# A second engine that fetches rows by plain DMAs in a message-passing kernel

## The chip, the cores and the metric

The kernel runs on one core of a Trainium2 chip. A core has a matrix engine (TensorE, PE in the profile), VectorE (DVE), ScalarE (ACT), GpSimd (POOL) and SyncE (SP), each with an instruction queue of its own that it works off in order, and sixteen DMA engines that they share. SBUF is the on-chip memory of 128 partitions, PSUM the memory that PE writes into.

The metric is the time of one execution on the device in microseconds. Before the change it is 3964.24 us, the median of three runs (3958.78 to 3966.85).

## The reference

One layer of a graph network over 12500 nodes and 400000 edges, sorted by their destination. A node has 64 scalars and 32 vectors of three components. For each edge, the rows of the source node are fetched, weighted by a small network of the edge's own 64 features, combined with four edge attributes and summed at the destination:

```python
h_s = s @ lin1_ws * a * _inv(S_IN)
h_v = jnp.einsum('nci,cd->ndi', v, lin1_wv) * a[:, :, None] * _inv(V_IN)
hid = jax.nn.silu(edge_scalars @ fc_w1 * _inv(R))
w = hid @ fc_w2 * _inv(FC_HID)
w1, w2, w3, w4, w5 = jnp.split(w, [64, 128, 160, 192], axis=-1)
es = h_s[edge_src]
ev = h_v[edge_src]
...
m_s1 = w1 * es * e0
m_s2 = w4 * jnp.einsum('eci,ei->ec', ev, e1) * _inv(3)
m_v1 = (w2 * es)[:, :, None] * e1[:, None, :]
m_v2 = w3[:, :, None] * ev * e0[:, :, None]
m_v3 = w5[:, :, None] * jnp.cross(ev, e1[:, None, :]) * _inv(2)
...
agg_s = jax.ops.segment_sum(mid_s, edge_dst, num_segments=n) * inv_nn
agg_v = jax.ops.segment_sum(mid_v, edge_dst, num_segments=n) * inv_nn
```

The sums go through a second linear map, a gate and a layer norm with the node's own row added.

## The kernel before

**Tiles and steps.** The 400000 edges are 3125 tiles of 128, one edge in each partition. A step works on a quad of four tiles; there are 782 steps. Six steps are a chunk of 24 tiles, whose 64 features per edge are loaded by SyncE in two DMAs (`load_chunk`, line 200, tile `es`). Ahead of the loop the table `h_tab` of 12500 rows, 160 floats or 640 bytes each, is computed and written to the chip's HBM.

**Where the rows come from.** `gather` (line 464) issues one indirect DMA per tile from GpSimd, 128 rows by the tile's indices, into `hg`, a tile for a quad out of a pool of four buffers (`deep`). For every 68th step from step 76 on, eleven in all (`own`, line 473), the rows come another way: `places` (line 477) loads the quad's indices as four rows of 128 into `at_bytes`, VectorE multiplies them by 640 (line 746), and `rows_of` (line 486) makes 32 jobs, each of which loads sixteen of these byte addresses into SyncE's registers (line 492) and issues sixteen DMAs of one row each (line 497) into `hq`, which has one buffer. `fetch_rows` (line 740) issues one job at every second step, so 32 jobs take 64 steps, and the quad is used by the step that they were made for.

**The order.** The scheduler is told to keep each engine's instructions in the order in which the code writes them, so the loop at line 874 is the order of every queue. In a step it issues: the loads that are due (`fetch`, for the quad four steps ahead), `fetch_rows`, the gather of this step, the matmuls of the edge weights into `pw` (line 510), a transposition for finished nodes if one is due (line 646), the one-hot rows of destinations (line 573), the products (lines 520 and 528, tile `pr`), the selection matrices (line 582, `sel`), the sums of the quad two steps before (`sum_up`, line 589, into `pa`), the first layer of the edge network for the quad two steps ahead (`hide`, line 459, and ScalarE's silu, line 461, tile `hid`), the second linear map of finished blocks (`output`, lines 613 and 616), and the transposition of summed blocks (`turn_blocks`, lines 598, 601 and 603, tile `tt`).

**What ScalarE does.** It copies a pair of finished blocks out of `pa` (line 795, tile `sa`, turned two steps later), the silu, the copies of `tt` and `os`, the reordering of edge attributes (line 556), the tanh and the square root of finished nodes (lines 648 and 673), and in steps 2 to 9 it clears the accumulator `acc` (line 433, two pieces a step). The PSUM tiles `ph`, `pt`, `po`, `pp` and `psc` take turns in two banks named `misc`; `pw` and `pa` have two buffers each.

**Finished nodes.** 25 jobs in the loop, of four tiles of 128 nodes each, and one behind it load `x`, turn the sums, gate, normalise and store (`finish`); the store is SyncE's (line 682) and waits for VectorE's `y` (line 679).

The functions that the diff touches:

Of the kernel before, what the change touches and what calls it, by code (L numbers as in the profile page):

```python
# [10 lines left out]
F32 = mybir.dt.float32  # L11
I32 = mybir.dt.int32
# [6 lines left out]
ENG = mybir.EngineType  # L19
PSUM = bass.MemoryType.PSUM  # L20

P = 128
# [3 lines left out]
D = S + V3  # L26
# [6 lines left out]
Q = 4  # L33
# [4 lines left out]
NF = 4  # L38
OWN = 68
BATCH = 16  # L40
EVERY = 2

MARGIN = 128
NO = 16
# [13 lines left out]
def gnn_kernel(  # L58
# [21 lines left out]
    nc = tc.nc  # L80
    N = x.shape[0]
# [19 lines left out]
        engines={ENG.PE, ENG.DVE, ENG.Activation, ENG.Pool, ENG.SP}))  # L101
# [33 lines left out]
    steps = []  # L135
# [92 lines left out]
    with tc.tile_pool(name="nodes", bufs=len(starts)) as nodes, tc.tile_pool(  # L228
        name="nodes_ps", bufs=6, space=PSUM
# [49 lines left out]
        for i in range(2):  # L279
            r = slice(S + i * V, S + (i + 1) * V)  # L280
# [23 lines left out]
        for half in range(2):  # L304
            r = slice(half * S, (half + 1) * S)
# [14 lines left out]
        for c0, cn, quarters, cq, xa, xz in loaded:  # L320
# [4 lines left out]
            first = c0 // P  # L325
            full = cn // P
            for t0 in range(0, nt, U):
                ps = nps.tile([P, U, P], F32, name="hp")
                for t in range(t0, min(t0 + U, nt)):
                    n = min(P, cn - t * P)  # L330
                    nc.tensor.matmul(ps[:n, t - t0], xa[:, t * P:t * P + n], l1,
                                     start=True, stop=True)
                k = min(U, full - t0)
# [3 lines left out]
                if t0 + k < nt <= t0 + U:  # L337
                    n = cn - full * P
# [4 lines left out]
            r = slice(0, P) if quarters == 4 else slice(S, S + V)  # L343
            by = l1z if quarters == 4 else l1[r, r]
            for u in range(-(-cq // P)):
                n = min(P, cq - u * P)
# [10 lines left out]
            if cn > full * P:  # L357
                n = cn - full * P
# [19 lines left out]
    for half in range(2):  # L378
        r = slice(half * S, (half + 1) * S)
# [21 lines left out]
    for to, part, pieces, w, r0, c0, by in maps:  # L401
        for k, piece in enumerate(pieces):
# [3 lines left out]
            m = terms.setdefault((to, part, four), len(terms))  # L406
            at_r = at_p * V
            r = l2[at_r:at_r + V, m, c0:c0 + w.shape[1]]
# [61 lines left out]
                in_offset=bass.IndirectOffsetOnAxis(ap=i, axis=0))  # L470
        return hg

    own = [n for n in range(OWN + 8, len(steps) - 4, OWN) if len(steps[n][2]) == Q]
    by_bytes = h_tab.rearrange("n d -> (n d)").bitcast(U8)
    row_bytes = 4 * D

    def places(pool, n):

        at_bytes = pool.tile([Q, P], I32, name="at_bytes")
        for k, (t, _, _) in enumerate(steps[n][2]):  # L480
            g, u = divmod(t, GT)
            with nc.allow_non_contiguous_dma(reason="the indices of one tile"):
                nc.sync.dma_start(at_bytes[k:k + 1], src[g][:, u:u + 1].rearrange("p u -> u p"))
        return at_bytes

    def rows_of(pool, at_bytes):

        hq = pool.tile([P, Q, D], F32, name="hq", bufs=1)
        flat_hq = hq.rearrange("p t d -> p (t d)").bitcast(U8)

        def job(t, p0):
            _, values = nc.values_load_multi_w_load_instructions(
                at_bytes[t:t + 1, p0:p0 + BATCH], engines=[ENG.SP], min_val=0,
                max_val=(N - 1) * row_bytes,
                skip_runtime_bounds_check_because="every entry of src is the index of a node")
            for p, v in enumerate(values, p0):
                nc.sync.dma_start(flat_hq[p:p + 1, t * row_bytes:(t + 1) * row_bytes],
                                  by_bytes[ds(v, row_bytes)][None])

        return hq, [lambda t=t, p0=p0: job(t, p0) for t in range(Q) for p0 in range(0, P, BATCH)]  # L500

    def weights(psum, hid, slots):

# [120 lines left out]
    def finish(fin, psum, t0, nt, p, most=NF):  # L624
# [50 lines left out]
        def norm():  # L675
# [14 lines left out]
    jobs = [(t, min(NF, tiles_of_nodes - LAST - t), P)  # L690
            for t in range(0, tiles_of_nodes - LAST, NF)]
    last_job = (tiles_of_nodes - LAST, LAST, N - (tiles_of_nodes - 1) * P)

    with tc.tile_pool(
        name="fin", bufs=1
    ) as fin, tc.tile_pool(
        name="mine", bufs=2
    ) as mine, tc.tile_pool(
        name="late", bufs=2
    ) as late, tc.tile_pool(name="edge", bufs=2) as edge, tc.tile_pool(  # L700
        name="deep", bufs=4
# [33 lines left out]
                for t, _, _ in tiles:  # L735
                    ahead(t)

        at_of, hq_of, rows_due = {}, {}, []

        def fetch_rows(n):  # L740

            for m in own:
                if n == max(1, m - OWN - 6):
                    at_of[m] = places(mine, m)
                if n == m - OWN + 2:
                    nc.vector.tensor_scalar_mul(at_of[m], at_of[m], float(row_bytes))
                    hq_of[m], jobs = rows_of(mine, at_of[m])
                    rows_due.extend((m, job) for job in jobs)
            if n % EVERY == 0 and rows_due:
                rows_due.pop(0)[1]()  # L750
            assert all(m > n for m, _ in rows_due)

        def hide(n):

# [112 lines left out]
        with in_order:  # L867
# [6 lines left out]
            for n, (c, i, tiles) in enumerate(steps):  # L874
# [5 lines left out]
                if n in checks:  # L880
                    checks[n]()
                fetch(n + 4)
                fetch_rows(n)
                hg = hq_of.pop(n) if n in own else gather(deep, [index(t) for t, _, _ in tiles])
                pw = weights(pw_ps, hids[c, i // 2], [(half, u - i // 2 * 4) for _, half, u in tiles])
# [34 lines left out]
            n = len(steps)  # L920
# [29 lines left out]
        with tc.For_i(0, n_redo, 1):  # L950
# [9 lines left out]
            with tc.For_i(0, n_again, 1) as g, tc.For_i(0, GT, 1) as k:  # L960
                t = g * GT + k
# [22 lines left out]
                r = edge.tile([P, 1], F32, name="r", bufs=1)  # L984
# [8 lines left out]
                first = nc.values_load(ends[0:1, 0:1], min_val=0, max_val=N - 1)  # L993
# [65 lines left out]
```

## Time and profile before

| | |
|---|---|
| median of three runs | 3964.24 us |
| profiled execution | 3954.57 us |
| its span, first to last instruction | 3952.6 us |
| mean granted TensorE clock | 0.969 |
| moved by DMA | 412.50 MB |
| GpSimd's gathers | 3081 |
| SyncE's DMAs of one row | 5632 |

The profile is of one execution. Its page gives busy time by engine; groups of instructions by line, with the count, the busy time, the mean length of one in ns and the idle time of the engine just before them with what ended it; other views list waits, the instructions in order of time, busy time by stretch, and the instructions of one line with their shortest, median and longest time. PEld is the weight load of PE. An engine name with a q (SPq, ACTq) is the engine's sequencer, which issues DMAs, loads registers and waits; that time is not counted as busy. A releaser of "issue" means that the engine waited for nothing that the profile shows.

### The profile page before, as it was taken

Reading aid. Unit: us, or ns where it says so; the run is one execution under the profiler, and the core shown is the slowest. Engines: PE = TensorE matmul, PEld = TensorE weight load, DVE = VectorE, ACT = ScalarE, POOL = GpSimd, SP = SyncE. Lnnn points to the kernel's source line nnn. Section 1 sums busy time; section 2 is a strip of 40 time slices with the busy share of each in tenths; the row PEclk is TensorE's granted clock in tenths of the full one; section 3 lists DMA queues with packets and bytes.
Section 4 is the critical chain, followed back from the end, with each engine's and each line's share of the span. In section 5 each row is a group of like instructions: output and inputs, shape, how many; then the busy total and the mean of one; then the engine's idle time right before and its main releaser. Section 6 shows DMA issues by size and latency. Waiting matters only on the chain. (4 is left out here: it accounts for less than half of the span.)

```text
span 3952.6 us, 58252 instructions
## 1 busy us (share of the span) xinstructions
PE 3649.2 (92%) x14269; PEld 1584.2 (40%) x14269; DVE 2415.6 (61%) x6524; ACT 894.0 (23%) x2480; POOL 2929.3 (74%) x3100
## 2 busy tenths in 40 slices
PE   5899999999999999999999999999999998999997
PEld 4343343343444344334344344344343443344343
DVE  5656565665665665656656656666665665666665
ACT  1322222222222222222222222222221221222222
POOL 4777777777777777777777777777777777777774
PEclk8999999999999999999999999999999999999999
DMA  8443444444444444344443443444443444444442
GB/s 230 97 103 90 108 105 96 108 103 105 100 96 110 103 97 108 95 116 96 102 110 86 110 110 89 108 100 100 108 106 90 109 103 105 100 100 108 100 109 55
DMA packets 243192, 412.50 MB, mean 104 GB/s; under 512 B 83069, under 2 KB 173497, under 8 KB 241945
## 3 DMA queue, kind: packets, MB, share of 16 engines
q0 software_dynamic: 150160, 262.93, 27.3%
q1 hardware_dynamic: 92246, 145.66, 15.8%
q8 instruction: 115, 1.88, 0.2%
q14 instruction: 235, 1.93, 0.2%
q10 hardware_dynamic: 436, 0.10, 0.0%
HBM read 392.43 MB, written 16.00 MB: 103 GB/s over the span
## 5 line engine op out<-in xcount | busy, mean ns | idle before, releaser
L468 POOL DMA_INDIRECT hg<-h_tab,idx x3081 | 2915.0, 946 | 949.5 <-issue 846.7
L510 PE MATMUL pw<-w,hid 128*128 128x448 f32 x3126 | 1363.3, 560 | 119.1 <-DVE sel L582 78.2
L589 PE MATMUL pa<-pr,sel 128*64 128x416 f32 x6250 | 1302.2, 539 | 3.1 <-DVE pw L573 2.9
L528 DVE TENSOR_TENSOR pr<-pw,hg 128x384 f32<-128x384 f32 x2313 | 1136.9, 547 | 0.0
L520 DVE TENSOR_TENSOR pr<-pw,hg 128x512 f32<-128x512 f32 x771 | 532.7, 691 | 876.8 <-DMA hg<-h_tab,idx 623.1
L510 PEld LDWEIGHTS pw<-w,hid 128*128 128x128 f32 x3126 | 555.2, 194 | 595.2 <-issue 461.6
L589 PEld LDWEIGHTS pa<-pr,sel 128*64 128x64 f32 x6250 | 388.0, 139 | 814.0 <-issue 803.6
L795 ACT COPY sa<-pa 128x416 f32<-128x416 f32 x521 | 263.3, 505 | 1205.7 <-PE pa L589 1190.5
L573 DVE TENSOR_TENSOR pw<-rel,iota 128x64 f32<-128x64 int16 x782 | 179.6, 230 | 543.5 <-PE pw L510 541.2
L459 PE MATMUL misc<-es,w 128*128 128x512 f32 (+1 forms) x784 | 450.2, 656 | 26.8 <-DVE rel L421 21.6
L461 ACT ACTIVATE hid<-misc 128x512 f32<-128x512 f32 x392 | 233.5, 596 | 778.4 <-PE misc L459 778.1
L598 PEld LDWEIGHTS misc<-ident,sa 128*128 128x128 f32 x2084 | 240.2, 141 | 318.7 <-issue 267.8
L613 PE MATMUL misc<-tt,l 128*96 128x256 f32 (+5 forms) x1474 | 343.6, 380 | 6.6 <-DVE y L659 6.0
L598 PE MATMUL misc<-ident,sa 128*128 128x128 f32 x2084 | 328.4, 280 | 8.3 <-DVE acc L776 3.8
L582 DVE TENSOR_TENSOR sel<-pw,eas 128x256 f32<-128x256 f32 x782 | 322.8, 413 | 0.0
L613 PEld LDWEIGHTS misc<-tt,l 128*96 128x96 f32 (+1 forms) x1474 | 225.2, 162 | 142.5 <-issue 73.9
L601 ACT COPY tt<-misc 128x192 f32<-128x192 f32 x521 | 164.7, 316 | 501.9 <-PE misc L598 482.6
L459 PEld LDWEIGHTS misc<-es,w 128*128 128x128 f32 x784 | 119.6, 192 | 293.8 <-issue 238.5
L621 DVE TENSOR_TENSOR acc<-acc,os 96x32 f32 x1042 | 194.6, 187 | 28.0 <-ACT os L616 9.6
L646 PE MATMUL misc<-ident,acc 96*128 96x96 f32 x196 | 36.6, 272 | 97.1 <-DVE pw L573 67.9
L603 ACT COPY tt<-misc 128x64 f32<-128x64 f32 x521 | 117.1, 225 | 0.0
L616 ACT COPY os<-misc 96x512 f32<-96x512 f32 (+2 forms) x67 | 38.2, 569 | 293.4 <-PE misc L613 286.7
(86 smaller groups left out, 608.6 us busy)
## 6 DMA issues: line engine op xcount, KB each, us to landing
es<-in_es_t_dram SPq DMA_DIRECT2D x258, 384.0 KB
hq<-h_tab SPq DMA_DIRECT2D x5632, 0.6 KB
hg<-h_tab,idx POOLq DMA_INDIRECT x3081
h_tab<-ht POOLq DMA_DIRECT2D x6, 1280.0 KB
xt<-in_x_dram SPq DMA_DIRECT2D x23, 320.0 KB
out_dram<-y SPq DMA_DIRECT2D x23, 320.0 KB
xv<-in_xv_t_dram SPq DMA_DIRECT2D x25, 187.5 KB
xs<-in_xs_t_dram SPq DMA_DIRECT2D x25, 125.0 KB
```

The source lines that it names most:

```text
L459: nc.tensor.matmul(ph[:k, c], w1[:k, :k], es[:k, t0 * P + c0 * P:t0 * P + c1 * P], start=True, stop=True)
L461: nc.scalar.activation(hid[:k, c], ph[:k, c], AF.Silu, scale=1.0 / math.sqrt(64))
L468: nc.gpsimd.indirect_dma_start(out=hg[:, t, :], out_offset=None, in_=h_tab, in_offset=bass.IndirectOffsetOnAxis(ap=i, axis=0))
L510: nc.tensor.matmul(pw[:, t:t + m, :NWT], hid[:m * S, c * P:(c + 1) * P], w2[:m * S, :m], start=True, stop=True)
L520: nc.vector.tensor_mul(two, pw[:, :n, :2 * S].rearrange("p t (k c) -> p t k c", k=2), hg[:, :n, None, :S].to_broadcast([P, n, 2, S]))
L528: nc.vector.tensor_mul(pr[:, :n, first:first + V3].rearrange("p t (i c) -> p t i c", i=3), pw[:, :n, None, 2 * S + k * V:2 * S + (k + 1) * ...
L582: nc.vector.tensor_mul(sel[:, :n], oh[:, :, None, :].to_broadcast([P, n, 4, W]), by_slot(tiles[0][0])[:, u:u + n, :, None].to_broadcast([P ...
L589: nc.tensor.matmul(pa[half * ROWS:(half + 1) * ROWS, :NPR], sel[:, t].rearrange("p k w -> p (k w)"), pr, start=start, stop=stop)
L598: nc.tensor.transpose(pt[:, four * P:four * P + k], sa[:k, c:c + P], ident[:k, :k])
L613: nc.tensor.matmul(po[:, k, :nb], l2[r, terms[to, part, four]], a[:, :nb], start=(n == 0), stop=(n == len(of) - 1))
L621: nc.vector.tensor_add(window, window, os[:, :, b])
L795: nc.scalar.copy(sa, pas.pop(j)[:, :NPR])
```

## The change

ScalarE gets quads of its own: step 122 and every 100th step after it, up to 722, seven in all. Their rows are fetched by 512 DMAs each from ScalarE's queue into a buffer `hq1`, by addresses in `at_bytes1`. GpSimd does not gather these quads. A batch of sixteen rows is issued in three steps, six, five and five rows, with the load of the sixteen addresses in the first of them; one such part stands in each step, behind `fetch` and SyncE's part and ahead of the step's other work. The 96 parts begin two steps after the quad before was used.

SyncE keeps its eleven quads. Its batch of sixteen is issued in two steps of eight rows, one part in every step, where all sixteen stood in every second step. The first quad of either engine begins at step 2 (SyncE's at step 10 before), its addresses at step 1.

```diff
-EVERY = 2
+SIDEWAYS = ((OWN, OWN + 8, 2), (100, 122, 3))
...
-    own = [n for n in range(OWN + 8, len(steps) - 4, OWN) if len(steps[n][2]) == Q]
+    own = {}
+    for k, (every, first, _) in enumerate(SIDEWAYS):
+        for n in range(first, len(steps) - 4, every):
+            while n in own:
+                n += 1
+            assert len(steps[n][2]) == Q
+            own[n] = k
...
-    def rows_of(pool, at_bytes):
-
-        hq = pool.tile([P, Q, D], F32, name="hq", bufs=1)
+    def rows_of(pool, at_bytes, k):
+
+        hq = pool.tile([P, Q, D], F32, name=f"hq{k}", bufs=1)
         flat_hq = hq.rearrange("p t d -> p (t d)").bitcast(U8)
-
-        def job(t, p0):
-            _, values = nc.values_load_multi_w_load_instructions(
-                at_bytes[t:t + 1, p0:p0 + BATCH], engines=[ENG.SP], min_val=0,
-                max_val=(N - 1) * row_bytes,
-                skip_runtime_bounds_check_because="every entry of src is the index of a node")
-            for p, v in enumerate(values, p0):
-                nc.sync.dma_start(flat_hq[p:p + 1, t * row_bytes:(t + 1) * row_bytes],
-                                  by_bytes[ds(v, row_bytes)][None])
-
-        return hq, [lambda t=t, p0=p0: job(t, p0) for t in range(Q) for p0 in range(0, P, BATCH)]
+        engine, queue = ((ENG.SP, nc.sync), (ENG.Activation, nc.scalar))[k]
+        parts = SIDEWAYS[k][2]
+        values = []
+
+        def job(t, p0, part):
+            if part == 0:
+                values[:] = nc.values_load_multi_w_load_instructions(
+                    at_bytes[t:t + 1, p0:p0 + BATCH], engines=[engine], min_val=0,
+                    max_val=(N - 1) * row_bytes,
+                    skip_runtime_bounds_check_because="every entry of src is the index of a node")[1]
+            for r in range(-(-BATCH * part // parts), -(-BATCH * (part + 1) // parts)):
+                queue.dma_start(flat_hq[p0 + r:p0 + r + 1, t * row_bytes:(t + 1) * row_bytes],
+                                by_bytes[ds(values[r], row_bytes)][None])
+
+        return hq, [lambda t=t, p0=p0, part=part: job(t, p0, part)
+                    for t in range(Q) for p0 in range(0, P, BATCH) for part in range(parts)]
...
-            for m in own:
-                if n == max(1, m - OWN - 6):
-                    at_of[m] = places(mine, m)
-                if n == m - OWN + 2:
+            for m, k in own.items():
+                start = max(2, max((o for o in own if own[o] == k and o < m), default=0) + 2)
+                if n == max(1, start - 8):
+                    at_of[m] = places(mine, m, k)
+                if n == start:
                     nc.vector.tensor_scalar_mul(at_of[m], at_of[m], float(row_bytes))
-                    hq_of[m], jobs = rows_of(mine, at_of[m])
-                    rows_due.extend((m, job) for job in jobs)
-            if n % EVERY == 0 and rows_due:
-                rows_due.pop(0)[1]()
-            assert all(m > n for m, _ in rows_due)
+                    hq_of[m], jobs = rows_of(mine, at_of[m], k)
+                    rows_due[k].extend((m, job) for job in jobs)
+            for queue in rows_due:
+                if queue:
+                    queue.pop(0)[1]()
+                assert all(m > n for m, _ in queue)
```

More of the change, by code (lines that the diff above doesn't have):

```diff
@@ L471, in gather, with places @@
         return hg
-    own = [n for n in range(OWN + 8, len(steps) - 4, OWN) if len(steps[n][2]) == Q]
+    own = {}
[5 more added lines that the diff above has]
+            own[n] = k
     by_bytes = h_tab.rearrange("n d -> (n d)").bitcast(U8)
     row_bytes = 4 * D
-    def places(pool, n):
-        at_bytes = pool.tile([Q, P], I32, name="at_bytes")
+    def places(pool, n, k):
+        at_bytes = pool.tile([Q, P], I32, name=f"at_bytes{k}")
         for k, (t, _, _) in enumerate(steps[n][2]):
@@ L736, in fetch @@
                     ahead(t)
-        at_of, hq_of, rows_due = {}, {}, []
+        at_of, hq_of, rows_due = {}, {}, ([], [])
         def fetch_rows(n):
-            for m in own:
-                if n == max(1, m - OWN - 6):
-                    at_of[m] = places(mine, m)
-                if n == m - OWN + 2:
-                    nc.vector.tensor_scalar_mul(at_of[m], at_of[m], float(row_bytes))
-                    hq_of[m], jobs = rows_of(mine, at_of[m])
-                    rows_due.extend((m, job) for job in jobs)
-            if n % EVERY == 0 and rows_due:
-                rows_due.pop(0)[1]()
-            assert all(m > n for m, _ in rows_due)
+            for m, k in own.items():
[3 more added lines that the diff above has]
+                if n == start:
+                    nc.vector.tensor_scalar_mul(at_of[m], at_of[m], float(row_bytes))
+                    hq_of[m], jobs = rows_of(mine, at_of[m], k)
[4 more added lines that the diff above has]
+                assert all(m > n for m, _ in queue)
         def hide(n):
```

## The prediction

> **What bounds the kernel now.** I read the busy shares first, then the costliest groups, then the waits of the engine that they point at.
>
> ```profile
> span 3952.6 us, 58252 instructions
> PE 3649.2 (92%) x14269; PEld 1584.2 (40%) x14269; DVE 2415.6 (61%) x6524; ACT 894.0 (23%) x2480; POOL 2929.3 (74%) x3100
> L582 DVE TENSOR_TENSOR sel<-pw,eas 128x256 f32<-128x256 f32 x782 | 322.8, 413 | 0.0
> L520 DVE TENSOR_TENSOR pr<-pw,hg 128x512 f32<-128x512 f32 x771 | 532.7, 691 | 876.8 <-DMA hg<-h_tab,idx 623.1
> ```
> ```profile
> L468 POOL DMA_INDIRECT hg<-h_tab,idx x3081: 942/946/1082, 61.3 to 3917.3; - x193
> ```
> ```profile
> POOL hg L468 <- issue: 846.7, 2778, 0.3
> POOL hg L468 <- DVE pr L528: 18.4, 50, 3.5
> ```
> By busy share PE looks like the bound (92%) and POOL does not (74%). The waits say otherwise. POOL issues 3081 gathers from 61.3 to 3917.3 us, one per (3917.3 - 61.3) / 3080 = 1.252 us: 0.946 us of work and 0.3 us before the next that the profile calls issue, 2778 times and never longer. It hardly ever waits for a free buffer: 18.4 us in 50 times, which includes the ordinary 0.3. DVE meanwhile waits 623 us for gathered rows. So **POOL's issue sets the end**: 782 steps (the count of the selection), four tiles in each, 4 x 1.252 = 5.01 us a step.
>
> PE comes close behind: 3649.2 / 782 = 4.67 us a step, and where the rows are there it runs faster still:
>
> ```profile
> 768.78 1.77 PE L510 MATMUL pw<-w,hid 128*128 128x448 f32 x4
> 773.43 1.67 PE L510 MATMUL pw<-w,hid 128*128 128x448 f32 x4
> 773.89 0.23 ACT L603 COPY tt<-misc 128x64 f32<-128x64 f32 x1
> ...
> 776.05 0.51 ACT L795 COPY sa<-pa 128x416 f32<-128x416 f32 x1 [1.93 <-PE pa L589]
> 776.58 0.66 PE L598 MATMUL misc<-ident,sa 128*128 128x128 f32 x4
> 777.07 1.67 PE L510 MATMUL pw<-w,hid 128*128 128x448 f32 x4
> ```
> From the first weight product to the third, two steps, are 8.29 us (columns: start, length). The mean 4.67 holds the longer steps with output and node work too.
>
> **The change, part by part.**
>
> *Gathers removed.* ScalarE's quads are steps 122, 222 and so on to 722: seven, 28 tiles. The eleven of SyncE stay. 28 x 1.252 = **35.1 us** off POOL, whose need falls to 3053 x 1.252 / 782 = 4.89 us a step. It is worth all of that only if PE, DVE and ACT can follow: PE's room is 4.89 - 4.67 = 0.22 us a step, 172 us over the run. That is the budget for all below.
>
> *ScalarE's issue.* No row shows a row DMA on ACT; SyncE's are the nearest, with ACT's own DMAs at the start as the other bound.
>
> ```profile
> L497 SPq MOVE hq<-h_tab x5632: 29/29/42, 120.3 to 3770.2; - x195
> L497 SPq DMA_DIRECT2D hq<-h_tab x5632: 222/228/332, 120.4 to 3770.2; - x195
> L492 SPq TENSOR_LOAD <-at_bytes x352: 982/1232/1862, 119.1 to 3762.5; - x176
> ```
> ```profile
> 1009.10 12.01 SPq L497 DMA_DIRECT2D hq<-h_tab  x32
> ```
> ```profile
> L265 ACTq DMA_DIRECT2D at<-in_attr_dram x1: 606/606/606, 3.4 to 3.4; - x1
> L268 ACTq DMA_DIRECT2D dt<-in_dst_dram x1: 305/305/305, 4.0 to 4.0; - x1
> ```
> On SP 32 DMAs with one load of sixteen addresses between them take 12.01 us: (12.01 - 1.23) / 32 = 0.34 us each. On ACT a DMA of one row took 0.305, one of 128 partitions 0.606; with the 0.03 of the move and the gap of some 0.07 (0.34 - 0.228 - 0.03) that makes 0.34 to 0.71. The moved DMA writes one partition, so I stay near the one-row end: 0.37. A batch is then 1.23 + 16 x 0.37 = 7.15 us in three steps: bursts of 1.85 (five rows, twice) and 3.45 us (the load and six rows). With ACT's present 894.0 / 782 = 1.14, its load is 2.38 + 1.14 = 3.5 of 4.89 us a step in the 7 x 96 = 672 steps that have a burst.
>
> *What hides the bursts.* A burst stands first in its step, behind the copy into tt that ended the step before. In the rows above that copy ends at 774.12 and ACT then waits 1.93 us for PE's sums before it copies sa. A burst of 1.85 lies in that hole; one of 3.45 overhangs by 1.5. Behind it are queued the copies of sa, the silu and the copies of tt; sa is turned two steps later, the silu is used two steps later, and PE can use the other misc bank meanwhile, so up to about one step of lateness stays off PE. I cost the overhang at nothing; without that cover it is 1.5 us in every third step, 0.5 a step, more than PE's room. In the node steps the tanh stands behind the burst, and DVE's gates wait for it: today 2.0 us in all for 98 tiles.
>
> ```profile
> L652 DVE SCALAR_TENSOR_TENSOR misc<-g,misc 128x64 f32<-128x64 f32 x98 | 21.6, 221 | 2.3 <-ACT g L648 2.0
> ```
> A third of those in burst steps (28) may now wait about 2 us, 56 us on an engine that is 39% idle: nothing.
>
> *The semaphores.* The trace's records show that the DMAs of SP and ACT take turns on the same eight semaphores in program order, and that each waits until the one eight places before it has landed. The first row here is SP held up by a transfer that ACT issued.
>
> ```profile
> SPq L682 <- DVE y L679: 271.4, 12, 33.2
> SPq L497 <- DMA es<-in_es_t_dram: 169.0, 141, 3.1
> ...
> SPq L239 <- DMA ws<-in_lin_ws_dram: 3.8, 1, 3.8
> ```
> ```profile
> L200 SPq DMA_DIRECT2D es<-in_es_t_dram x260: 465/517/1851, 74.0 to 3869.5; - x130
> L682 SPq DMA_DIRECT2D out_dram<-y x26: 384/420/429, 395.0 to 3944.4; - x26
> ```
> So ACT's rows of a step wait for SP's eight of that step to land, and SP's next for ACT's: SP can no longer run steps ahead, and what holds SP holds ACT's compute behind its rows. The 32 DMAs at 0.34 without a pause bound one row's landing at 8 x 0.34 = 2.7 us; 13.3 rows a step then need 13.3 / 8 x 2.7 = 4.5 us, under 4.89: it just fits. The loads of es (130 pairs) are slower: they held SP 169.0 / 141 = 1.2 us on the mean, 3.1 at most, against ACT's 4.89 - 3.5 = 1.4 us to spare. The stores of the output wait for DVE's y; ACT's next burst then comes some 4 us late (the store, a load of 1.23, landing up to 2.7), 26 times, about every 30 steps, in which PE's room is 6.6 us. Bounds for both together: 0, and 130 x 672 / 782 = 112 loads under bursts x 3.1 = 347 less the 172 of room, 175 us. The mean row is nearest to the low end: **+4 us**.
>
> *The start.* In steps 2 to 9 ACT also clears acc, two copies of 1.5 us a step.
>
> ```profile
> 84.00:116.00 32.00, 32.00 (x124) 12.75 (x123) 26.00 (x73) 27.69 (x32) 23.80 (x26) 1.00 0.36 87
> ```
> ```profile
> L433 ACT COPY acc<-zero 96x1568 f32<-96x1568 f32 x16 | 23.2, 1501 | 0.0
> ```
> (A stretch: its length, then busy time of PE, PEld, DVE, ACT, POOL.) PE is full here and ACT busy for 27.69 of 32 us. Eight bursts, of 6, 5, 5, 6, 5, 5, 6 and 5 rows, add 43 x 0.37 + 3 x 1.23 = 19.6 us; 47.3 does not fit in 32, and the chain runs about 15 us late. POOL goes on while it has buffers: four of hg, so three quads or 15 us ahead at most, part of which is already used then. Bounds 0 and 15; I take **+6 us**, near the middle, as both rows say that it is full.
>
> *SyncE's edits.* Eight rows a step for sixteen every other: the same rows, hidden behind POOL. Its first quad and ScalarE's fetch their addresses at step 1, eight DMAs, and DVE scales them at step 2.
>
> ```profile
> L483 SPq DMA_DIRECT2D at_bytes<-in_src_dram x44: 552/590/604, 75.5 to 3426.0; - x44
> ```
> ```profile
> L520 DVE TENSOR_TENSOR pr<-pw,hg x771: 291/691/694, 82.2 to 3921.3; 128x512 f32<-128x512 f32 x193
> ```
> 8 x 0.59 from 75.5 ends at 80.2; DVE's first product, of step 0, is at 82.2, so its step 2 comes later than the landing: nothing, and inside POOL's lead in any case.
>
> [...]
>
> ```profile
> q0 software_dynamic: 150160, 262.93, 27.3%
> q1 hardware_dynamic: 92246, 145.66, 15.8%
> ```
> The DMA engines are 43% busy while POOL issues without a pause, so the sum stays.
>
> **The sum.** -35.1 + 4 + 6 = -25 us on the profiled execution's 3954.57: 3929.5. The median of the runs, 3964.24, stands 9.7 above that execution; on it I forecast **3939 us**.
>
> **The rivals.**
>
> *Held by es (slower).* Place: ACT's rows behind the loads of es. Six steps need 6 x 4.67 = 28.0 us on PE and 29.3 on POOL; 1.3 us of hold per load are free. If a hold reaches PE with h, 112 (h - 1.3) is lost; it eats 35.1 - 6 = 29 us from h = 1.56 on. At h = 2.2, halfway between SP's mean and longest wait, +101 - 29 = +72: 4036. For it: SP's 3.1, and SP tied to ACT starts es later. Against: the mean of 1.2, and the lateness that ACT can hide. 0.16.
>
> *ACT bound by its issue.* At the 0.64 us of the wide start DMA with its move, a batch is 11.5 us, 3.8 + 1.14 = 5.0 a step: over 4.89, the old pace at best, and with 0.1 to 0.3 of waits a step over 672 steps 4000 to 4150. Against: 0.305 for a single row. 0.05.
>
> *PE takes over.* The room of 172 us is a mean; output groups come in lumps:
>
> ```profile
> 749.84 5.25 PE L613 MATMUL misc<-tt,l 128*96 128x256 f32 x22
> ```
> If such lumps, a quad of ScalarE's (a lead of 5 us for POOL) and an overhang meet, POOL's four buffers fill and it stops. At 17 such stops of 1 us beside the sum, -8: 3956. 0.14.
>
> *All of it.* The start is absorbed by POOL's lead: -35, 3929. 0.20.
>
> **How the numbers follow.** The forecast has 0.45, own range 3931 to 3948; with the rivals' 0.16, 0.05, 0.14 and 0.20 that is one. 0.2% (8 us) is about what a measurement can tell from no change. Faster: 0.45 + 0.20 + 0.05 of PE takes over = 0.70; the other 0.09 of it is the same; slower 0.16 + 0.05 = 0.21. The range reaches from below the full gain, 3922, into the slower cases, 3990: outside are some 0.14 of those above and 0.05 below.
>
> **What would show it.** Right: 3053 gathers still at 1.25 us; 18 products that read rows not gathered; ACT's row DMAs at 0.34 to 0.40; POOL's waits for DVE at a few us in the run and about 6 more before 200 us; sums on PE still back to back. Wrong: POOL waits for buffers through the whole run (PE or ACT sets the pace); PE waiting for hid, sa or misc behind ACT, and ACT's rows waiting for es (the slower rival); ACT's row DMAs above 0.6 us.

## The result, and the profile after

The change made the kernel slower: 4452.12 us, the median of five runs (4445.93 to 4458.55), against 3965.51 us for the kernel before beside it, a ratio of 1.1227, 95% interval [1.1215, 1.1239]. The forecast was 3939 us, the range 3922 to 3990. The experiments below stand beside a kernel before of 3957.67 or 3957.65 us, the two that ran last (bound four steps back; bound two steps back with early loads) beside one of 3965.36. In eight earlier runs of six of these kernels the kernel before itself took 5269 to 5338 us, for a reason that is not known, so they are told apart from the others.

The head of the profile after, the gathers, and the group of PE whose idle time grew most:

```profile
span 4450.4 us, 65685 instructions
PE 3743.6 (84%) x14269; PEld 1637.1 (37%) x14269; DVE 2445.7 (55%) x6531; ACT 884.9 (20%) x2480; POOL 2901.5 (65%) x3072
L468 POOL DMA_INDIRECT hg<-h_tab,idx x3053 | 2887.2, 946 | 1475.7 <-issue 833.1
L459 PE MATMUL misc<-es,w 128*128 128x512 f32 (+1 forms) x784 | 500.0, 723 | 452.3 <-DMA es<-in_es_t_dram 378.2
```

The 28 gathers are gone, and one still takes 0.946 us. No engine became the bound by its work: every engine's share of busy time fell. Some of the waits of the profile after (columns: total, times, longest):

```profile
PE misc L459 <- DMA es<-in_es_t_dram: 378.2, 61, 11.4
POOL hg L468 <- DVE pr L539: 309.6, 126, 11.4
POOL hg L468 <- DMA idx<-in_src_dram: 132.2, 16, 12.0
DVE y L670 <- DMA xt<-in_x_dram: 210.3, 20, 18.7
ACT hid L461 <- PE misc L459: 1011.5, 289, 70.4
ACT sa L808 <- DMA hq<-h_tab: 395.8, 141, 5.3
```

The same view of the kernel before has a few microseconds for es and for xt:

```profile
PE misc L459 <- DMA es<-in_es_t_dram: 4.7, 2, 2.6
DVE y L659 <- DMA xt<-in_x_dram: 2.6, 1, 2.6
```

PE's first layer of the edge network now waits for the edge features, 61 times and for up to 11.4 us; POOL stops because its four buffers are full (DVE's products, 309.6 us) and because the indices idx, which SyncE loads as well, come late (132.2 us). POOL is no longer what sets the pace. **PE's time adds up**: its busy time grew by 3743.6 - 3649.2 = 94.4 us, its idle time by (4450.4 - 3743.6) - (3952.6 - 3649.2) = 403.4, together the 497.8 us by which the span grew. Of the idle time the wait for es is 378.2 - 4.7 = 373.5. The late xt adds to it by way of DVE, for whose y PE stands 62.1 us; in turn the 78.2 us that PE waited for DVE's sel before are down to 5.8.

One such stop, in the order of time, on the kernel after (start, length, engine, line; in brackets the idle time before it):

```profile
2004.43 1.15 SPq L200 DMA_DIRECT2D es<-in_es_t_dram  x2
2007.14 10.82 SPq L507 DMA_DIRECT2D hq<-h_tab  x16
2011.45 2.04 PE L459 MATMUL misc<-es,w 128*128 128x512 f32 x2 [8.36 <-DMA es<-in_es_t_dram]
2013.29 3.19 PE L521 MATMUL pw<-w,hid 128*128 128x448 f32 x4
2013.54 0.60 ACT L461 ACTIVATE hid<-misc 128x512 f32<-128x512 f32 x1 [9.83 <-PE misc L459]
2013.61 1.57 ACTq L507 DMA_DIRECT2D hq<-h_tab  x5
2018.02 0.41 SPq L647 DMA_DIRECT2D xt<-in_x_dram  x1
2018.52 1.11 SPq L200 DMA_DIRECT2D es<-in_es_t_dram  x2
2021.46 0.38 DVE L670 SCALAR_TENSOR_TENSOR y<-misc,half_at,xt 128x160 f32<-128x160 f32 x1 [18.65 <-DMA xt<-in_x_dram]
2023.51 0.94 POOL L468 DMA_INDIRECT hg<-h_tab,idx  x1 [10.39 <-DVE pr L539]
```

SyncE asks for es at 2004.43, and PE, which is already there, gets it at 2011.45. ScalarE's queue has its rows behind the silu that needs this layer, so it issues none until 2013.61. SyncE's sixteen rows took 10.82 us where 32 took 12.01 before, and it comes to xt, for which DVE has been waiting, only at 2018.02, after ScalarE's rows. That is a ring: PE waits for SyncE's load, SyncE for a place behind ScalarE's rows, ScalarE for PE.

A stop costs more than its length. The four products of the second weight matrix take 3.19 us behind it, against 1.67 before. By stretch (length, busy time of PE, PEld, DVE, ACT, POOL, then the granted clock), first 10 us behind the stop, then 30 us of the kernel before:

```profile
2020.00:2030.00 10.00, 5.90 (x16) 2.17 (x16) 6.17 (x18) 0.77 (x3) 4.97 (x6) 0.50 0.50 130
```
```profile
2000.00:2030.00 30.00, 27.67 (x103) 10.81 (x103) 19.44 (x54) 6.23 (x22) 22.68 (x25) 0.94 0.39 95
```

After the stop the granted clock is 0.50, where the kernel before has 0.94; over the whole span it is 0.915 against 0.969, and the trace's clock records have 0.50 for 756 us of it against 250 before. I put PE's 94 us of longer matmuls down to that; the 3.19 against 1.67 us and the 0.50 agree. In this stop PE stands from 2003.10 to 2011.45, works up to 2016.48, and works again from 2024.10 on; the clock is 0.50 from 2006.3 to 2016.6 and from 2020.0 to 2033.6, and 1.00 between and behind them, so the way back took some 5 us of work the first time and 9.5 the second.

### The profile page after: what moved, and what is told of

Same layout as the page of the kernel before. It is cut to its first block, busy times and chain, and to the rows that moved or that the text cites. A ratio compares the mean times of both kernels' runs of the same rounds, so it can differ in the third digit from the quotient of the medians.

```text
span 4450.4 us, 65685 instructions
## 1 busy us (share of the span) xinstructions
PE 3743.6 (84%) x14269; PEld 1637.1 (37%) x14269; DVE 2445.7 (55%) x6531; ACT 884.9 (20%) x2480; POOL 2901.5 (65%) x3072
## 3 DMA queue, kind: packets, MB, share of 16 engines
q0 software_dynamic: 148816, 260.63, 22.5%
q1 hardware_dynamic: 96278, 145.68, 13.6%
## 5 line engine op out<-in xcount | busy, mean ns | idle before, releaser
L521 PE MATMUL pw<-w,hid 128*128 128x448 f32 x3126 | 1379.9, 566 | 10.9 <-DVE sel L593 5.8
L459 PE MATMUL misc<-es,w 128*128 128x512 f32 (+1 forms) x784 | 500.0, 723 | 452.3 <-DMA es<-in_es_t_dram 378.2
L521 PEld LDWEIGHTS pw<-w,hid 128*128 128x128 f32 x3126 | 568.8, 198 | 496.3 <-issue 453.7
L459 PEld LDWEIGHTS misc<-es,w 128*128 128x128 f32 x784 | 129.7, 208 | 714.0 <-issue 659.8
L624 PE MATMUL misc<-tt,l 128*96 128x256 f32 (+5 forms) x1474 | 385.4, 414 | 7.4 <-DVE y L670 6.8
L609 PE MATMUL misc<-ident,sa 128*128 128x128 f32 x2084 | 332.5, 283 | 68.5 <-DVE y L670 62.1
L624 PEld LDWEIGHTS misc<-tt,l 128*96 128x96 f32 (+1 forms) x1474 | 253.4, 181 | 178.5 <-issue 94.2
L670 DVE SCALAR_TENSOR_TENSOR y<-misc,half_at,xt 128x160 f32<-128x160 f32 x98 | 37.6, 384 | 213.3 <-DMA xt<-in_x_dram 210.3
```

The source lines that it names most:

```text
L459: nc.tensor.matmul(ph[:k, c], w1[:k, :k], es[:k, t0 * P + c0 * P:t0 * P + c1 * P], start=True, stop=True)
L521: nc.tensor.matmul(pw[:, t:t + m, :NWT], hid[:m * S, c * P:(c + 1) * P], w2[:m * S, :m], start=True, stop=True)
L609: nc.tensor.transpose(pt[:, four * P:four * P + k], sa[:k, c:c + P], ident[:k, :k])
L624: nc.tensor.matmul(po[:, k, :nb], l2[r, terms[to, part, four]], a[:, :nb], start=(n == 0), stop=(n == len(of) - 1))
```

## The experiments

**Three theories.** A: the two queues hold each other up through the eight semaphores that they share, and the loads of es and xt come late. B: ScalarE's own time for its rows (3584 at some 0.33 us) delays its copies and the silu. C: eight semaphores are too few for two queues, in whatever order. A step's code has SyncE's loads first, so A needs an explanation of why es is late at all; that came from the compiled program and is told below.

**ScalarE fetches alone.** SyncE's quads are gathered by POOL again, 3097 gathers:

```diff
     for k, (every, first, _) in enumerate(SIDEWAYS):
+        if k == 0:
+            continue
```

> ScalarE's seven quads stay as in the change; SyncE fetches no rows at all (its eleven quads go back to GpSimd, 3097 gathers). Theory A, the order of the shared semaphores: in the program as compiled, SyncE's loads of es stand behind ScalarE's rows of up to two steps later, so they are issued only when PE already needs them; without SyncE's rows in between they stand about seven steps ahead again. A expects GpSimd's pace, 3097 x 1.252 + 99 = 3976 us, 3970 to 4000, and PE's waits for es below 30 us. Theory B, ScalarE's time: the address loads and row DMAs hold up its copies and silu. B expects them to do so here too: above 4300. Theory C, eight semaphores for both queues are too few in any order: in between, 4050 to 4300, and ScalarE still waiting for rows of its own for hundreds of us.

3991.31 us, ratio 1.0082 [1.0065, 1.0099]. PE's wait for es is 0.5 us. Sixteen gathers more than before are worth 16 x 1.252 = 20 us, so ScalarE's rows by themselves cost some 14 us, not 500. B falls here, and the time lies below C's range too.

**ScalarE busy without DMAs.** Its quads are gathered by POOL, and each part is four copies of 128x512 in place of rows:

```diff
+            if k == 1:
+                for _ in range(4):
+                    nc.scalar.copy(idle, zero.to_broadcast([P, 512]))
...
-                hg = hq_of.pop(n) if n in own else gather(deep, [index(t) for t, _, _ in tiles])
+                hg = hq_of.pop(n) if own.get(n) == 0 else gather(deep, [index(t) for t, _, _ in tiles])
```

> ScalarE issues no rows: in their place it makes four copies of 128 x 512 per step (some 2.1 us a step, 672 steps, 1.4 ms as the address loads and row DMAs together), and its seven quads are gathered by GpSimd as before the change. SyncE's rows stay as in the change. A and C expect the time of before or the start's few us more: 3960 to 3985. B expects the loss of the change: above 4300.

3956.94 us, ratio 0.9998 [0.9988, 1.0008]. The page of that run:

```profile
PE 3653.5 (92%) x14269; PEld 1585.3 (40%) x14269; DVE 2420.8 (61%) x6531; ACT 2454.2 (62%) x5168; POOL 2929.4 (74%) x3100
```

1560 us more on ScalarE cost nothing, at the start of the run neither. SyncE's edits (eight rows a step, an earlier first quad) are in this kernel too, and they cost nothing.

**The order of the loads.** The DMAs of SyncE and ScalarE take the same eight semaphores in turn: in the trace of the change 6252 DMAs of SyncE and 3589 of ScalarE report to them, 1230 or 1231 to each. Each waits until the one eight places before has landed: of the 9833 pairs of neighbours on a semaphore, 9820 have a completion of the earlier on record before the issue of the later is done, and 13 have none. The order of those turns across the two queues is not that of the code: numbered by semaphore and round, each queue's DMAs stand in its own order without exception, but the two are interleaved otherwise than the code has them. (The trace gives this for the change, and its row of the table below; the rows of the other kernels are read from the compiled programs, not from a profile.) A load of es written in step s is needed by PE in step s + 2. Let a be the last step whose rows of ScalarE stand before it in the turns: then the load is 2 - (a - s) steps ahead of its use. In the change a - s is +2 for 53 of 98 loads, so there SyncE cannot ask for es until ScalarE has reached the step that needs it.

**A dependence that binds ScalarE's first row of a step to SyncE's last row of an earlier one** moves the place of es in the turns. One step before:

```diff
...
+                if k == 0:
+                    last_sp.append(sent.ins.name)
+                elif len(last_sp) > 8 and fresh:
+                    tc.add_manual_dep(sent.ins, last_sp[-9], mybir.DependencyInfo(
+                        mybir.DependencyClass.Sync, mybir.DependencyReason.DATA))
+                    fresh.clear()
```

> The same instructions as the change; one dependence more per step: the first of ScalarE's rows of a step waits until the last of SyncE's rows of the step before has landed. With it the compiled order of the semaphores is that of the code (the load of es ahead of ScalarE's rows of the same step, where it stood behind those of two steps later). A expects most of the loss gone: 3930 to 4000, es waits of PE below 60 us. B expects no gain: 4400 to 4500. C expects a part: 4100 to 4400, because the two queues still wait for each other's landings, now with one wait more.

4049.42 us, ratio 1.0227 [1.021, 1.0244]: 400 us of the loss are gone; the time lies 49 us above A's range and 51 below C's. PE has no wait for es left. What is left (ScalarE's idle time holds its own issue of the rows, up to 3.45 us a part by the prediction's row times):

```profile
ACT sa L816 <- DMA hq<-h_tab: 969.4, 254, 11.6
POOL hg L468 <- DVE pr L547: 140.5, 97, 6.0
```

**Two steps before** (`last_sp[-17]`) and **the same step** (`last_sp[-1]`):

> The kernel of e6 once more, on another chip: in its first run the kernel before took 5269 us, where it takes 3958 elsewhere, and engines waited over 1000 us for releases that the profile puts down to nothing of this core, so that run tells nothing of this change. Expectations as then. R1 (ScalarE waits for SyncE's rows; loosening helps): 3965 to 4035. R2 (SyncE's loads are still late; loosening makes them later): 4070 to 4250.

> The kernel of e7 once more, for the same reason. R1: 4070 to 4250, with more idle time of ScalarE put down to row DMAs than in the code order. R2: 3970 to 4035.

4007.25 us, 1.012 [1.0104, 1.0135], and 4151.68 us, 1.0487 [1.0471, 1.0503], both as R1 had them (ScalarE waits for SyncE's rows, so loosening helps). Bound in the same step, ScalarE's silu is late behind its rows, and POOL stops (first rows); bound two steps before, there is less of that, and a little waiting for es (second):

```profile
ACT hid L461 <- DMA hq<-h_tab: 572.9, 77, 17.2
POOL hg L468 <- DVE pr L547: 238.9, 127, 9.4
```
```profile
ACT sa L816 <- DMA hq<-h_tab: 838.9, 206, 11.6
POOL hg L468 <- DVE pr L547: 61.3, 67, 10.2
PE misc L459 <- DMA es<-in_es_t_dram: 25.9, 16, 2.8
```

**Four steps before** (`last_sp[-33]`). A dependence could help just by pacing ScalarE's rows. This one waits for less, and in the turns the loads of es fall back to where they stand in the change:

> The kernel bound four steps back, a third time, wanted beside a kernel before near 3960 us. R1 (the place of es and xt behind ScalarE's rows costs the time): 4300 to 4460 us, PE waits for es 200 us or more. R2 (the added wait helps by pacing): 3960 to 4030 us, PE's wait for es below 60 us.

4423.08 us, ratio 1.1152 [1.113, 1.1174]: the loss is back.

```profile
PE misc L459 <- DMA es<-in_es_t_dram: 373.4, 64, 9.4
```

The loads of es between steps 130 and 720, by how many steps they stand ahead of their use in the turns, for the kernels with the loads four steps ahead in the code:

| kernel | steps ahead: loads | PE's wait for es, us | time, us |
|---|---|---|---|
| the change | 0: 53, 1: 7, 2: 28, 3 to 5: 10 | 378.2 (61 times) | 4452 |
| bound four steps back | 0: 53, 1: 7, 2: 28, 3 to 5: 10 | 373.4 (64) | 4423 |
| bound two steps back | 1: 1, 2: 81, 3 to 5: 16 | 25.9 (16) | 4007 |
| bound one step back | 2: 2, 3: 86, 4 to 7: 10 | none | 4049 |
| bound in the same step | 3: 6, 4: 78, 5 to 8: 14 | none | 4152 |
| ScalarE alone | 2: 1, 3: 4, 6 to 13: 93 | 0.5 (1) | 3991 |

The two kernels with the same places of es have the same wait. Load by load, in the trace of the change: of the 53 loads with no lead 46 stop PE, for 317 us together; of the 7 with a lead of one step 3 do, for 12 us; of the 28 with two steps 2 do, for 2 us; of the other 10 none does. (The remaining stops lie outside steps 130 to 720.) That the place in the turns makes es late, and that this is most of the loss, is shown. C falls as the cause of that part: bound two steps back, the same rows of both queues on the same eight semaphores take 4007 us. The other end of the table has another price: the tighter ScalarE's rows are bound to SyncE's, the longer ScalarE stands before them, with its copies and silu behind, and the longer the time (4007, 4049, 4152).

**Loads eight steps ahead in the code**, without a dependence:

```diff
+            for k in range(1, 8):
+                fetch(k)
...
-                fetch(n + 4)
+                fetch(n + 8)
```

> The change with all loads of es, idx and eat placed four steps earlier in the code, same buffers. In the compiled order es then stands on the mean some two to three steps of ScalarE's rows ahead of its use, where it stood at none to two steps. A expects PE's waits for es to fall from 378 us to below 150 and the time to 4100 to 4300; the loads of x for finished nodes (210 us of DVE's waits) stay late. B expects 4400 to 4500. C expects 4300 to 4450.

4368.58 us, ratio 1.1036 [1.1017, 1.1054]: 70 us above A's range, and inside C's.

```profile
PE misc L459 <- DMA es<-in_es_t_dram: 66.1, 14, 8.6
DVE y L670 <- DMA xt<-in_x_dram: 389.0, 21, 32.5
PE misc L788 <- DMA xs<-in_xs_t_dram: 61.6, 7, 13.0
```

The wait for es falls by 312 us and the time by 84 only (76 when each kernel is set against its own kernel before), while DVE's wait for xt grows from 210.3 to 389.0. I read it so: the turns do not hold SyncE at a fixed distance, it falls back until its next load, here xt or xs, is just late, and the load that is late is whichever comes first. That fits A as well as C; what decides between them is the order, above.

**Both: bound two steps back, loads eight steps ahead.**

> The kernel bound two steps back with loads eight steps ahead, a third time. Late loads as the rest of the loss: 3925 to 3975 us, PE's wait for es gone. ScalarE standing at its rows as the rest of the loss: 3985 to 4030 us.

4000.53 us, ratio 1.0087 [1.0067, 1.0107]. Nearly all es loads stand six steps ahead now (81 of 99), and the row for es is gone; the loss beside the own kernel before is 35 us where it was 50 (the intervals of the two ratios just overlap).

```profile
ACT sa L816 <- DMA hq<-h_tab: 808.7, 235, 14.2
POOL hg L468 <- DVE pr L547: 88.5, 68, 10.0
DVE y L678 <- DMA xt<-in_x_dram: 49.8, 18, 4.6
```

So late loads of es are at most a small part of the rest of the loss. What is left of it goes with ScalarE standing at its rows: the copy of sa comes behind them, up to 14.2 us, far more than one part's issue and nearly three steps, and POOL's buffers fill now and then (88.5 us). That a steady load on ScalarE cost nothing and this does is in line with it, and so is ScalarE alone, whose copies of sa come behind its rows for 570.1 us, at most 7.1, at a cost of 14 us. That it is the landings in the shared turns which make it stand is argued, not shown. A rival stands beside it: xt is still late here (third row; 2.6 us before), since only es, the indices and the edge attributes were loaded earlier. It can't be all, because bound one step back xt waits for 1.2 us only and the loss is 92. Giving ScalarE's rows semaphores of their own would show it and was not tried.

**SyncE alone, more quads.** No rows on ScalarE; SyncE takes a quad every 56 steps at ten rows a step (13 quads, 8 gathers fewer than before), or every 52 at eleven (14 quads).

```diff
-SIDEWAYS = ((OWN, OWN + 8, 2), (100, 122, 3))
+SIDEWAYS = ((56, 64, BATCH),)
+ROWS_A_STEP = 10
...
-                if queue:
+                for _ in range(min(ROWS_A_STEP, len(queue))):
                     queue.pop(0)[1]()
```

> The kernel of e8 once more, for the same reason. Theory A: ratio 0.9965 to 0.9985 (8 gathers fewer, 10 us). The rival, SyncE behind and its loads late: above 1.000.

> The kernel of e9 once more, for the same reason. Theory A: ratio 0.9950 to 0.9975 (12 gathers fewer, 15 us). The rival: above 1.000, PE waiting for es.

3961.92 us, 1.001 [1.0001, 1.0019], and 4141.32 us, 1.0466 [1.0452, 1.048]. Already at ten rows a step the 8 gathers' 10 us are given back, at eleven far more:

```profile
PE misc L460 <- DMA es<-in_es_t_dram: 78.1, 32, 8.0
```
```profile
PE misc L460 <- DMA es<-in_es_t_dram: 215.4, 51, 8.9
DVE y L671 <- DMA xt<-in_x_dram: 161.0, 18, 12.9
```

The symptom is the same without a second queue that issues: SyncE alone has too much to do to keep its lead, while eight rows a step left it all of its lead (3.9 us of waiting for es in the kernel with copies). A wait is not always a loss by its whole length: the 78.1 us at ten rows stand beside some 14 lost. Theory A's gain of 0.15 to 0.35% for 56 did not come, the rival's late SyncE did. No version tried beats the kernel before.

**The runs beside a kernel before of 5269 to 5338 us.** They are of the same six kernels, ahead of the runs told above; only the ratio to their own kernel before can be read in them. The first four and their expectations:

> The code order of the semaphores, loosened: the first of ScalarE's rows of a step waits for the last of SyncE's rows of two steps before, where it was one step. In the compiled order the load of es then stands level with ScalarE's rows of the same step, one step later than in the code order, two earlier than in the change. What is left of the loss in the code order (4049 against 3958) has two readings. R1: ScalarE waits for SyncE's rows; loosening lets it go earlier: 3965 to 4035. R2: SyncE's loads are still late; loosening makes them later: 4070 to 4250.

> The same, tightened: the first of ScalarE's rows of a step waits for the last of SyncE's rows of the same step, so that es stands two steps ahead of them, four ahead of its use. R1: ScalarE waits longer, 4070 to 4250, with more idle time before its copies put down to row DMAs than in the code order. R2: the loads come earlier, 3970 to 4035.

> No rows on ScalarE; SyncE fetches every 56th quad, thirteen instead of eleven, ten rows in each step. Eight gathers fewer than before: 8 x 1.252 = 10 us off GpSimd. Theory A: nothing is queued in front of any load that another engine must release, so the gain comes whole, ratio 0.9965 to 0.9985. A rival: SyncE, with 10 x 0.324 + 0.63 x 1.23 + 0.2 = 4.2 of about 4.95 us a step, falls behind and its loads come late: above 1.000.

> The same with every 52nd quad, fourteen, eleven rows in each step: twelve gathers fewer than before, 15 us. Theory A: ratio 0.9950 to 0.9975, if SyncE's 11 x 0.324 + 0.69 x 1.23 + 0.2 = 4.6 us a step still leaves it ahead. The rival, SyncE's loads late: above 1.000, with PE waiting for es.

5603.65, 5522.73, 5732.10 and 5924.13 us, beside 5268.89: ratios 1.0616 [1.058, 1.0652], 1.047 [1.0435, 1.0506], 1.0868 [1.0832, 1.0903] and 1.1238 [1.1193, 1.1282]. The times that were expected for the first two do not apply beside such a kernel before, and their order is turned round against the runs above, so nothing follows from them; the ratios of the other two lie above 1.000, as the rival had it and theory A did not. Then the two last kernels, twice each:

> ScalarE's first row of a step waits for SyncE's last row of four steps before. In the compiled order the load of es then stands behind ScalarE's rows of up to two steps later in most chunks (a-s = +2, as in the change itself), where the kernel bound two steps back had a-s = 0 and took 4007 us. Theory R1 (what costs is the place of es and xt behind ScalarE's rows): the loss comes back, 4300 to 4460 us, and PE waits for es 200 us or more. Theory R2 (the added wait helps by itself, because it paces ScalarE's rows): a looser wait costs less waiting, so 3960 to 4030 us, below the 4007 of two steps, with PE's wait for es below 60 us.

> The kernel bound two steps back (4007 us, a-s = 0), with the loads of es, indices and weights eight steps ahead in place of four. If the rest of its loss (50 us above before) is loads that come just late, it falls to 3925 to 3975 us, and PE's wait for es (25.9 us) is gone. If the rest is ScalarE standing at its rows until a transfer of SyncE's eight places before has landed, it stays within 3985 to 4030 us: the wait of tanh at its rows' line does not depend on when es is asked for.

> The kernel bound four steps back, again, beside a kernel before that takes its usual time near 3960 us. R1 (the place of es and xt behind ScalarE's rows costs the time): 4300 to 4460 us, PE waits for es 200 us or more. R2 (the added wait helps by pacing): 3960 to 4030 us, PE's wait for es below 60 us.

> The kernel bound two steps back with loads eight steps ahead, again, beside a kernel before near 3960 us. Late loads as the rest of the loss: 3925 to 3975 us, PE's wait for es gone. ScalarE standing at its rows as the rest of the loss: 3985 to 4030 us.

Four steps back 5991.35 and 5974.08 us, ratios 1.1228 [1.1182, 1.1275] and 1.1177 [1.1117, 1.1238]; two steps back with early loads 5608.26 and 5606.43 us, 1.051 [1.0472, 1.0548] and 1.0503 [1.0446, 1.056], beside 5336.78 and 5338.10. The kernel in whose turns es stands behind ScalarE's rows is the slower one here too.

## Why the prediction was wrong

**The step that failed** is the one on the semaphores. It put the turns down as going "in program order" and took +4 us, from the row in which SyncE's rows wait for es, 1.2 us on the mean. The sharing was right (1230 or 1231 DMAs of the two queues on each of the eight semaphores); the order was not. In code order a load stands ahead of every row of its own and later steps; in the compiled change 53 of 98 stand behind ScalarE's rows of the very step that needs them. No row of the profile before shows the order of the turns across two engines, because only one engine issued in the loop; I took the code's order for it. (The one row in the prediction's fence that shows a wait across the queues is the third, ws, not the first.) The wait that I priced, the second row here, hardly changed:

```profile
SPq L507 <- DMA hq<-h_tab: 1059.1, 857, 17.2
SPq L507 <- DMA es<-in_es_t_dram: 131.1, 95, 4.1
```

Rows behind es are 131.1 / 95 = 1.4 us. What I did not price is the reverse, es behind rows that ScalarE has not issued. What is new is the first row, SyncE's rows behind other rows, which was next to nothing before:

```profile
SPq L497 <- DMA hq<-h_tab: 0.9, 4, 0.3
```

My upper bound of 175 us held one transfer's landing; what is waited for is an engine's turn, which hangs on PE. With the other terms left as forecast, the term measures 497.8 + 35.1 - 6 = 527 us in place of 4.

**The order is not all of it.** Bound one step back, most loads of es stand three steps ahead of their use, which is the order that the prediction took, and the time is 4049.42, outside the forecast range as well; with the best order found it is 4000.53. The prediction had said that what holds SyncE holds ScalarE's compute behind its rows, and priced only the holds by es. So +4 us was too little for every order tried: with the best one the term would be 35 + 35.1 - 6 = 64. How much of that is the added dependence itself is open.

**The rival "Held by es"** named the right place and the right sign, but by the mechanism of the row above: it set in at 1.56 us of hold per load and gave 4036. The hold was 1.4, under that point, and the time 4452. One line of its case points at what happened (SyncE tied to ScalarE starts es later), without a price.

**What bounds it.** POOL's issue at 1.252 us a gather was not put to a proof of its own: no kernel took gathers away without adding another load. ScalarE alone, with sixteen more, is compatible with it (20 of its 34 us).

**The issue on ScalarE** was sized nearly right, though the terms named for it, 0.305 + 0.03 + 0.07, make 0.41; the low bound of 0.34 was SyncE's pace. Of the kernel after:

```profile
L507 ACTq DMA_DIRECT2D hq<-h_tab x3584: 234/235/842, 88.3 to 4120.7; - x200
L502 ACTq TENSOR_LOAD <-at_bytes x224: 1178/1196/1806, 87.0 to 4108.1; - x112
```

The five rows from 2013.61 took 1.57 us, so (1.57 - 0.235) / 4 = 0.33 from one to the next, against 0.37; the load of addresses 1.20 against 1.23. "ACT bound by its issue" falls with it.

**SyncE's edits at nothing**: right, by the kernel with copies. **Hidden bursts at nothing**: that kernel bears it out for ScalarE's time as such, 1560 us against some 3584 x 0.33 + 224 x 1.20 = 1450 for the rows, but its copies come evenly; with real bursts, ScalarE alone has 14 us that the gathers do not account for. **The start at +6**: up to 250 us POOL's waits for DVE's products are 6.1 us in the change and 5.0 before, so the term was too large by about 5.

**"PE takes over" and "All of it"** were never reached, since no kernel in which both queues fetch ran at POOL's pace of 3053 gathers. The prediction kept its sum because the DMA engines were 43% busy while POOL issued; after the change they are 36% busy on the mean (22.5 + 13.6 + 0.3). With the best order found, 4000.53 beside 3965.36, the second issuer saved less than nothing all the same.

**What would show it wrong** was listed aptly in part: POOL waiting for buffers through the whole run is the 309.6 us. PE waiting for es itself was not on the list.

## What to carry to other kernels

A DMA queue that runs ahead of the compute is a resource (PE waited 4.7 us for es where SyncE ran ahead, 378.2 where it did not): before a second engine is made to issue DMAs, ask whether its completions share semaphores with the first, and in which order the compiled program, not the code, takes them. Be wary of letting an engine that computes in order issue DMAs on which another queue's prefetches wait: here stalls of its compute became late loads (61 waits for es) and came back as the next stalls. When a prefetch is late, asking for it earlier may only move the lateness to the next load, as here, while what holds the queue is still there.

## What was not expected

- 1560 us of extra copies on ScalarE (62% busy in place of 23%) left the time where it was, 0.9998 [0.9988, 1.0008]; even the few microseconds at the start that A and C allowed for did not come.
- SyncE with rows alone goes from no cost at eight rows a step over 1.001 at ten to 1.0466 at eleven: its lead begins to go at ten (32 waits for es) and most of the cost comes with the eleventh.
- The stops cost twice: 373.5 us of waiting for es came with 94.4 us of slower matmuls.
